# Attention and a gated feed-forward on one core: quadrants filled in the heads' order, the division of y and its parts spread over more steps, low halves summed at other steps

## The chip, the cores and the metric

The kernel runs on one core of a Trainium2 chip. A core has TensorE (PE in the profile), VectorE (DVE), ScalarE (ACT), GpSimd (POOL) and SyncE (SP), which issues DMAs. Every engine works through its own queue in order, and engines wait for each other on semaphores. The metric is the device time of one execution in microseconds (us), here the median of three runs.

## The reference

There are 4 batches of 1024 tokens with 256 channels, 16 heads of 16 channels, all in float32. The weights of attention are binarized: their signs times the mean of their absolute values per row.

```python
def _binlinear(x, W, b):
    Wb = _binarize(W)                    # mean(|W|) per row, times sign(W)
    return einsum('btc,oc->bto', x, Wb) + b
...
q, k, v = (split_heads(_binlinear(x, W, b)) for W, b in ((Wq, bq), (Wk, bk), (Wv, bv)))
att = softmax(einsum('bhtd,bhsd->bhts', q, k) * Dh ** -0.5)
y = einsum('bhts,bhsd->bhtd', att, v)    # heads joined to B, T, C
attention = _binlinear(y, Wp, bp)
...
h = silu(tlin(x, w1, s1)) * tlin(x, w2, s2)           # 256 -> 1024, ternary weights times a scale
h = gelu(tlin(h, h1, sh1))                            # 1024 -> 1024
h = gelu(tlin(h, h2, sh2))
ffn = tlin(h, w3, s3)                                 # 1024 -> 256
...
x = x + layernorm(attention(layernorm(x)))
x = x + layernorm(ffn(layernorm(x)))
```

## The kernel before

One program holds attention (`attention(True)`) and then the feed-forward part (`mlp`), which works in 8 blocks of 512 tokens and is not changed. A flag that `weight_jobs` computes tells whether the feed-forward weights have any low bits; for these inputs the short path runs.

**Blocks and steps.** A unit `u` is a batch and a group of four heads (16 units), a block is a unit and a half of its queries (512; 32 blocks, `blk`), and a block has 8 steps, one for each 128 keys. So there are 256 steps, `s`, and 10 steps ahead of them. In a step PE forms, for the four heads, the scores of the second pass (L664: three matmuls for each head, the third subtracts the row's maximum), the exponentials are taken by ACT (L674), and PE multiplies them by v (L690), in two groups of y matmuls. Beside this PE forms the scores of the first pass (L618, two matmuls per head), ten steps ahead, and DVE takes the maximum of each (L627). The four heads of a group stand in four quadrants of 32 partitions, so that their matmuls run side by side. A step is written as five slots. Head 0 and head 1 begin at slot 0, head 2 one slot later, head 3 three slots later (`BEGIN`). All scores go through seven PSUM banks (`through`), which `bank()` gives out by planned times.

**Jobs.** Everything else is a job that is put by hand at a place `(step, 0 or 1)`: 0 is issued after slot 2, 1 after the last slot. Jobs of one place are issued in the order in which they were placed. Those that matter here:

- `spread(u)` (L506), at step `16u - 16`: 24 DMAs on SP's queue bring q (high and low piece) and k of the next unit into the quadrants. They go quadrant by quadrant, in the order 2, 3, 0, 1. The unit's first pass begins six steps later. The spread of the first unit uses SP's and ACT's queues, before the steps begin.
- `fetch_y` (L705): ACT copies a block's y out of PSUM. `turn_y` (L710) transposes it on DVE, `divide` takes a reciprocal on DVE (L715) and multiplies on GpSimd (L716, into `yn`), `return_y` transposes back on DVE (L731) and issues four DMAs on SP into `yT`. They stand at steps 1 and 2 behind the block.
- `project_jobs(b, half)`: for each half batch, when its last heads are done. Two pieces (ACT takes the high part, L522, DVE the low part, L523), two projections (PE, L536; ACT's copy, L545; four GpSimd operations each, L550 and L551), four measured tiles (DVE, L162 and L163, the last with `rstd` on GpSimd, L151 and L153), and four finishing tiles (GpSimd, L565 and L568).
- `batch_jobs(b)`: measured tiles and norm tiles (GpSimd, L399) of the next batch, its transposes (L411, with L416 on ACT and L419 on DVE) and its values (L428, L434).
- `group_jobs(grp)`: the projections of q and k for two units (L469, L476), split into pieces by GpSimd (L482, L483).
- `combine` and `shift`: GpSimd arranges the maxima of a block (L636 to L638) for PE's transposes (L644).
- `weight_jobs`: 44 sums of low halves on GpSimd (`gather`, L817 and L818), each of a 128 x 512 piece of the feed-forward weights. For 28 of them SP loads the piece first, two ahead (L823): the load for the next but one waits until the piece has been read.

The places where these jobs come from:

```python
place((at - 6, 0), lambda u=u: spread(u))
...
at = (((b + 1) * NG - 1) * NQ + half + 1) * STEPS + (6, 10)[half]
...
at = (blk + 1) * STEPS + 1
...
while at % STEPS not in (3, 7) and job not in last_gathers:
```

Of the kernel before, what the change touches and what calls it, by code (L numbers as in the profile page):

```python
# [30 lines left out]
F32 = mybir.dt.float32  # L31
# [3 lines left out]
AF = mybir.ActivationFunctionType  # L35
ALU = mybir.AluOpType
# [10 lines left out]
def sandwich_kernel(  # L47
# [23 lines left out]
    nc = tc.nc  # L71
    B, T, C = x.shape
    F = w1T.shape[1]
    KC = C // P
    NF = F // P
    DH = C // HEADS
    NG = HEADS // 4
    NT = T // P
    NQ = T // 512
# [76 lines left out]
    def moments(n, tag):  # L156
        return scratch[-1].tile([P, n, 2], F32, tag=f"mvp{n}", name=f"mvp_{tag}")
# [73 lines left out]
    def attention(signs):  # L231


        with ExitStack() as actx:
# [11 lines left out]
            def bank():  # L246
                b = min(free_at, key=free_at.get)
                clock["PE"] = max(clock["PE"], free_at.pop(b))
                return b
# [105 lines left out]
            STEPS = NT  # L355
# [21 lines left out]
            def half_tile(name, dtype=F32):  # L377

                return a2.tile([P, NT // 2, C], dtype, tag="xn", name=name, bufs=3)
# [109 lines left out]
            def spread(u, queues=(nc.sync,)):  # L489

                grp, i = divmod(u, 2)
                q_of[u] = [
                    a2.tile([P, T], F32R, tag=f"qs{n}", name=f"qs{n}_{u}") for n in range(2)
                ]
                k_of[u] = a2.tile([P, T], F32R, tag="ks", name=f"ks_{u}")
                for g in (2, 3, 0, 1):
                    rows = slice(64 * i + 16 * g, 64 * i + 16 * g + 16)
                    for half in range(2):
                        to = slice(32 * g + 16 * half, 32 * g + 16 * half + 16)
                        for dst, src in (  # L500
                            (q_of[u][0], pieces_of[grp, True][0]),
                            (q_of[u][1], pieces_of[grp, True][1]),
                            (k_of[u], pieces_of[grp, False][half]),
                        ):
                            queue = queues[half % len(queues)]
                            queue.dma_start(dst[to, :].bitcast(F32), src[rows, :].bitcast(F32))  # L506
# [3 lines left out]
            def project_jobs(b, half):  # L510

                y_pieces, y_by = [], []

                def piece(k):

                    if k == 0:
                        y_pieces[:] = [half_tile(f"y{j}_{b}_{half}", F32R) for j in range(2)]
                    hi, lo = (
                        y.rearrange("p n c -> p (n c)")[:, bass.ts(k, 512)] for y in y_pieces
                    )  # L520
                    y, factor = yT_of[b, half][:, k, :], alpha_sb[:, 2, k : k + 1]
                    y_by.append(nc.scalar.activation(hi, y, AF.Copy, scale=factor).ins)  # L522
                    y_by.append(nc.vector.scalar_tensor_tensor(  # L523
                        lo, y, factor, hi.bitcast(F32), ALU.mult, ALU.subtract
                    ).ins)

                def project(m):
                    t = bank()
                    ys = [
                        y.rearrange("p n c -> p (n c)").rearrange("p (k t) -> p k t", k=KC)  # L530
                        for y in y_pieces
                    ] if signs else [yT_of[b, half]]
                    for i in range(2):
                        for k in range(KC):
                            for j, y in enumerate(ys):
                                put(t, nc.tensor.matmul(  # L536
                                    through[:, t, bass.ts(i, C)],
                                    y[:, k, bass.ts(2 * m + i, P)], w_in["p"][:, k, :],
                                    start=(k == 0 and j == 0),
                                    stop=(k == KC - 1 and j == PIECES - 1),  # L540
                                ), y_by)
                    if m == 0:
                        z_of[b, half] = half_tile(f"z_{b}_{half}")
                    z = z_of[b, half][:, 2 * m : 2 * m + 2, :]
                    got([t], "ACT", nc.scalar.copy(  # L545
                        z, through[:, t, :].rearrange("p (n c) -> p n c", n=2)
                    ))
                    for i in range(2):
                        if signs:
                            nc.gpsimd.tensor_mul(z[:, i, :], z[:, i, :], az_bc)  # L550
                        nc.gpsimd.tensor_add(z[:, i, :], z[:, i, :], bz_bc)  # L551

                def measure_tile(i):
                    if i == 0:
                        z_of["moments"] = moments(NT // 2, f"z{b}_{half}")
                    mv = z_of["moments"]
                    measure_one(mv, i, z_of[b, half][:, i, :], f"z{b}_{half}")
                    if i == NT // 2 - 1:
                        z_of["moments"] = mv, rstd(mv[:, :, 1], NT // 2, f"z{b}_{half}")

                def finish_tile(i):
                    z = z_of[b, half][:, i, :]
                    to = x_sb[:, b, half * NT // 2 + i, :]
                    mv, rs = z_of["moments"]
                    nc.gpsimd.tensor_scalar(  # L565
                        z, z, mv[:, i, 0:1], rs[:, i : i + 1], ALU.subtract, ALU.mult
                    )
                    nc.gpsimd.tensor_add(to, to, z)  # L568

                return [lambda k=k: piece(k) for k in range(KC) if signs], [  # L570
                    lambda m=m: project(m) for m in range(2)
                ], [
                    lambda i=i: measure_tile(i) for i in range(NT // 2)
                ], [lambda i=i: finish_tile(i) for i in range(NT // 2)]
# [160 lines left out]


            jobs = {}

            def place(at, job):
                jobs.setdefault(at, []).append(job)  # L740

            first = -STEPS - LEAD
            for b in range(1, B):
                norms, turns, values = batch_jobs(b)
                at = b * NG * NQ * STEPS + first
                for i, job in enumerate(norms):
                    place((at - 32 + i // 2, i % 2), job)
                for i, job in enumerate(turns):
                    place((at - 18 + i // 2, i % 2), job)

                for i, job in enumerate(values):
                    place((at - first - STEPS + 3 + 2 * i, 0), job)
            for u in range(1, B * NG):
                at = u * NQ * STEPS + first
# [3 lines left out]
                place((at - 6, 0), lambda u=u: spread(u))  # L758
            for b in range(B):
                for half in range(2 if b < B - 1 else 1):  # L760
                    at = (((b + 1) * NG - 1) * NQ + half + 1) * STEPS + (6, 10)[half]
                    pieces, projects, measures, finishes = project_jobs(b, half)
                    for i, job in enumerate(pieces):
                        place((at - 2, i), job)
                    for i, job in enumerate(projects):
                        place((at + i, 1), job)
                    for i, job in enumerate(measures):
                        place((at + 3 + i // 2, i % 2), job)
                    for i, job in enumerate(finishes):
                        place((at + 5 + i, 0), job)  # L770

            *tile_jobs, turn = middle_input()
            for n in range(8):
# [6 lines left out]
            for blk in range(BLOCKS):  # L780
                at = (blk + 1) * STEPS + 1
                hurry = blk == BLOCKS - 1
                for job, when in (
                    (turn_y, (at, 1)), (divide, (at + 1, 0)), (return_y, (at + 1, 1))
                ):
                    when = (total, 1) if hurry else when
                    place(when, lambda blk=blk, job=job: job(blk))
# [64 lines left out]
            loads, gathers, last_gathers = weight_jobs()  # L852
# [14 lines left out]
            at = 44  # L867
            for job in gathers + last_gathers:
                if job is last_gathers[0]:
                    at = max(at, free + 6)  # L870
                while at % STEPS not in (3, 7) and job not in last_gathers:
                    at += 1
                place((at, 1), job)
                at += 1
# [55 lines left out]
            for s in range(first, total + 1):  # L930
                steps = slots(s)
                for i, (some, parts) in enumerate(steps):
# [3 lines left out]
                    at = clock["PE"]  # L936
# [358 lines left out]
    with small_ones.Else():  # L1295
        attention(False)
        mlp("G", True, wp_all)
# [43 lines left out]
```

## Time and profile before

| | |
|---|---|
| median of three runs | 1618.42 us (1615.15 to 1619.83) |
| the profiled execution | 1616.46 us, its span 1614.6 us |
| mean granted TensorE clock | 0.982 |
| TensorE, VectorE, ScalarE, GpSimd busy | 95%, 67%, 51%, 26% |
| L627, maxima on VectorE | 1024 of 680 ns, 642.8 us |
| L674, exponentials on ScalarE | 1024 of 604 ns, 546.9 us |
| L710 and L731, transposes of y on VectorE | 32 of 704 and 32 of 702 ns |
| L716, the division on GpSimd | 32 of 619 ns |
| L817 and L818, a sum of low halves on GpSimd | 44 of 610 and 1281 ns |
| L506, DMAs of the spreads on SP's queue | 372, landing after 2.4 us (median) |

A line of a timeline gives the start and the length in us, the engine, the line of the kernel, the operation, what it writes and reads, how often in a row, and in brackets how long the engine stood idle before it and what ended that. A line of the list of waits gives who waited for whom, the total in us, how many times, and the longest. A line of a table of stretches gives the stretch, its length, the busy time of PE, PE's weight loads, DVE, ACT and POOL, the granted clock, the DMA share and GB/s.

### The profile page before, as it was taken

How to read it: one execution, taken by the hardware profiler on the slowest of the kernel's cores; microseconds unless marked ns; L12 is line 12 of the kernel's file. 1: busy time of each engine (PE TensorE's matmuls, PEld its weight loads, DVE VectorE, ACT ScalarE, POOL GpSimd, SP SyncE). 2: the span in 40 equal slices, each digit the busy share in tenths (PEclk: the TensorE clock that was granted, in tenths of full speed). 3: DMA queues.
4: the chain of work that ended last, by engine and by line, in shares of the span. 5: the costliest groups of instructions: out<-in, count | busy, mean ns of one | idle time of the engine just before them, and what ended most of it. 6: DMA issues, size and time to landing. Idle time of an engine off the chain costs nothing.

```text
span 1614.6 us, 31662 instructions
## 1 busy us (share of the span) xinstructions
PE 1533.2 (95%) x12964; PEld 982.4 (61%) x12964; DVE 1074.6 (67%) x1964; ACT 822.8 (51%) x1481; POOL 427.9 (26%) x574
## 2 busy tenths in 40 slices
PE   4599999998999999999989999999999999999997
PEld 3354444543445444444434468888888888888886
DVE  4588878888887888887879743644545454545443
ACT  2067677676777667776767771223232323232221
POOL 1011322565132555325631142120202020202011
PEclk9689999999999999999999999999999999999999
DMA  1502332212221232132123003000000000000000
GB/s 56 108 3 46 66 90 47 44 27 64 57 60 35 57 64 59 32 73 60 27 54 96 8 10 128 1 13 1 14 1 14 1 14 1 13 1 14 1 13 16
DMA packets 35707, 60.11 MB, mean 37 GB/s; under 512 B 10208, under 2 KB 21728, under 8 KB 35552
## 3 DMA queue, kind: packets, MB, share of 16 engines
q1 hardware_dynamic: 29568, 44.35, 12.9%
q0 software_dynamic: 3792, 11.54, 2.4%
q10 hardware_dynamic: 2192, 2.10, 0.6%
q8 instruction: 104, 1.70, 0.4%
q14 instruction: 51, 0.42, 0.1%
HBM read 24.40 MB, written 4.19 MB: 18 GB/s over the span
## 4 chain that ended last, share of the span: by engine, by line
PE 78%; DVE 8%; POOL 5%; ACT 4%; SPq 2%; issue 2%; DMA 1%; ACTq 0%; DVEq 0%
PE g L1075 29%; PE y L690 12%; PE through L664 11%; PE through L618 9%; PE p L1075 7%; DVE nm L627 5%; PE fzp L1189 4%; PE through L469 2%; ACT e L674 2%; SPq L506 2%; PE through L428 1%; PE through L644 1%; POOL z L565 1%; POOL xn L399 1%; PE through L536 1%
## 5 line engine op out<-in xcount | busy, mean ns | idle before, releaser
L627 DVE TENSOR_REDUCE nm<-through 128x1 f32<-128x512 f32 x1024 | 642.8, 680 | 127.9 <-PE through L618 66.7
L674 ACT ACTIVATE e<-through 128x512 f32<-128x512 f32 x1024 | 546.9, 604 | 182.9 <-PE through L664 168.2
L618 PE MATMUL through<-ks,qs 32*128 32x512 f32 x2048 | 467.3, 450 | 22.8 <-DMA ks<-h1b_sb 17.5
L664 PE MATMUL through<-qs,ks 32*128 32x512 f32 x2048 | 446.5, 439 | 21.7 <-DVE nm L627 16.2
L664 PE MATMUL through<-nmT,ones_r 32*128 32x512 f32 x1024 | 352.2, 454 | 0.4 <-ACT nmT L651 0.4
L690 PE MATMUL y<-e,v 128*32 128x256 f32 x4096 | 324.1, 394 | 0.0
L618 PEld LDWEIGHTS through<-ks,qs 32*128 32x128 f32 x2048 | 218.7, 187 | 127.8 <-issue 81.9
L664 PEld LDWEIGHTS through<-qs,ks 32*128 32x128 f32 x2048 | 206.2, 185 | 52.7 <-DVE nm L627 28.1
L1075 PE MATMUL g<-g,h_sb 128*128 128x512 f32 x1024 | 235.7, 390 | 0.0
L1075 PEld LDWEIGHTS g<-g,h_sb 128*128 128x128 f32 x1024 | 191.7, 188 | 39.5
L664 PEld LDWEIGHTS through<-nmT,ones_r 32*128 32x128 f32 x1024 | 139.6, 184 | 92.4 <-issue 89.5
L690 PEld LDWEIGHTS y<-e,v 128*32 128x32 f32 x4096 | 86.5, 108 | 171.1 <-issue 151.7
L1118 ACT ACTIVATE g2f<-g,sh_sb 128x512 f32<-128x512 f32 x64 | 44.2, 691 | 200.4 <-PE g L1075 173.0
L1118 ACT ACTIVATE g1f<-g,sh_sb 128x512 f32<-128x512 f32 x64 | 44.1, 691 | 170.1 <-PE g L1075 166.8
L151 POOL TENSOR_SCALAR ve_fz<-mvp_fz 128x4 f32<-128x4 f32 (+1 forms) x8 | 1.9, 233 | 470.7 <-DVE mvp_fz L163 470.7
L1075 PE MATMUL g<-h,h1a_sb 128*128 128x512 f32 x512 | 126.4, 389 | 0.0
L1075 PE MATMUL g<-h,h1b_sb 128*128 128x512 f32 x512 | 126.4, 389 | 0.0
L1045 DVE CAST g<-g2f 128x512 fp32r<-128x512 f32 x64 | 27.7, 433 | 142.0 <-ACT g2f L1118 142.0
L1075 PE MATMUL p<-xnT_sb,w_sb 128*128 128x512 f32 x512 | 118.0, 390 | 1.7 <-DVE hf L1151 1.7
L1075 PEld LDWEIGHTS p<-xnT_sb,w_sb 128*128 128x128 f32 x512 | 95.5, 188 | 22.0 <-DVE hf L1151 2.1
L1075 PEld LDWEIGHTS g<-h,h1b_sb 128*128 128x128 f32 x512 | 96.1, 188 | 20.0
L1075 PEld LDWEIGHTS g<-h,h1a_sb 128*128 128x128 f32 x512 | 96.1, 188 | 19.9
(173 smaller groups left out, 1486.5 us busy)
## 6 DMA issues: line engine op xcount, KB each, us to landing
qs<-h1b_sb SPq DMA_DIRECT2D x248, 64.0 KB, 2.4
ks<-h1b_sb SPq DMA_DIRECT2D x124, 64.0 KB, 2.4
wraw<-in_dram SPq DMA_DIRECT2D x28, 256.0 KB, 2.9
h_sb<-in_dram POOLq DMA_DIRECT2D x4, 1024.0 KB, 8.2
yT<-yt SPq DMA_DIRECT2D x112, 32.0 KB, 2.0
out_dram<-x_sb SPq DMA_DIRECT2D x7, 512.0 KB, 2.8
x_sb<-in_dram SPq DMA_DIRECT2D x3, 1024.0 KB, 5.6
w_sb<-in_dram POOLq DMA_DIRECT2D x3, 1024.0 KB, 7.7
```

The lines of the kernel that those rows point to most:

```text
L399: engine.tensor_scalar(xn_of[half][:, i, :], x_sb[:, b, half * NT // 2 + i, :], mv[:, i, 0:1], rs[:, i : i + 1], ALU.subtract, ALU.mult,)
L469: put(t, nc.tensor.matmul(through[:, t, :], w_in[tag][:, k, bass.ts(c, P)], xnT[i][:, k, bass.ts(j, 512)], start=(k == 0 and i == 0), stop ...
L506: queue.dma_start(dst[to, :].bitcast(F32), src[rows, :].bitcast(F32))
L618: put(t, nc.tensor.matmul(through[:, t, :], q_of[u][n][rows, bass.ts(qt, P)], k_of[u][rows, bass.ts(j, 512)], start=(n == 0), stop=(n == 1),))
L627: got([t], "DVE", nc.vector.tensor_reduce(nm_of[blk][:, n4, j, g : g + 1], through[:, t, :], AX.X, ALU.max, negate=True))
L664: t, nc.tensor.matmul(through[:, t, :], lhs, rhs, start=(n == 0), stop=(n == 2)),
L674: exps.append(got([t], "ACT", nc.scalar.activation(e_of[s, g], through[:, t, :], AF.Exp)))
L690: nc.tensor.matmul(y_of[blk][32 * g : 32 * g + 32, cols], v_sb[n // 2][:, n % 2, :, :].rearrange("p h d -> p (h d)")[:, bass.ds((4 * g4 + ...
L1045: nc.vector.tensor_copy(hi, full)
L1075: nc.tensor.matmul(out[c], wk, src[j][:, k, :], start=(k == 0 and i == 0 and j == 0), stop=(k == n_k - 1 and i == len(ws) - 1 and j == 1),)
L1118: nc.scalar.activation(g, ps, AF.Gelu, scale=scale[:, c : c + 1])
L1189: nc.tensor.matmul(out_ps[i][:, :C], g2[j][:, k, bass.ts(i, P)], wk, start=(k == 0 and n == 0 and j == 0), stop=(k == NF - 1 and n == len( ...
```

## The change

The spreads fill the quadrants in the order 0, 1, 2, 3. The high and the low piece of y become jobs of their own, half a step apart, and all jobs of a half batch stand one step later. `turn_y` stands half a step later, `divide` half a step, `return_y` a whole step. The sums of low halves go to steps 0, 4 and 7 of eight instead of 3 and 7, but to none of the steps that are marked as busy: those with norm tiles, with finishing tiles, and those that follow a projection. No operation is added or removed.

```diff
-                for g in (2, 3, 0, 1):
+                for g in range(4):
...
-                def piece(k):
-
-                    if k == 0:
+                def piece(k, low):
+
+                    if k == 0 and not low:
                         y_pieces[:] = [half_tile(f"y{j}_{b}_{half}", F32R) for j in range(2)]
...
-                    y_by.append(nc.scalar.activation(hi, y, AF.Copy, scale=factor).ins)
-                    y_by.append(nc.vector.scalar_tensor_tensor(
-                        lo, y, factor, hi.bitcast(F32), ALU.mult, ALU.subtract
-                    ).ins)
+                    if low:
+                        y_by.append(nc.vector.scalar_tensor_tensor(
+                            lo, y, factor, hi.bitcast(F32), ALU.mult, ALU.subtract
+                        ).ins)
+                    else:
+                        y_by.append(nc.scalar.activation(hi, y, AF.Copy, scale=factor).ins)
...
-                return [lambda k=k: piece(k) for k in range(KC) if signs], [
+                return [
+                    (k + low, lambda k=k, low=low: piece(k, low))
+                    for k in range(KC if signs else 0) for low in range(2)
+                ], [
...
+            busy = set()
...
                     place((at - 32 + i // 2, i % 2), job)
+                    if i >= NT // 2:
+                        busy.add(at - 32 + i // 2)
...
-                    at = (((b + 1) * NG - 1) * NQ + half + 1) * STEPS + (6, 10)[half]
+                    at = (((b + 1) * NG - 1) * NQ + half + 1) * STEPS + (7, 11)[half]
                     pieces, projects, measures, finishes = project_jobs(b, half)
-                    for i, job in enumerate(pieces):
-                        place((at - 2, i), job)
+                    for i, job in pieces:
+                        place((at - 2 + i // 2, i % 2), job)
                     for i, job in enumerate(projects):
                         place((at + i, 1), job)
+                        busy.add(at + i + 1)
...
                     for i, job in enumerate(finishes):
                         place((at + 5 + i, 0), job)
+                        busy.add(at + 5 + i)
...
-                    (turn_y, (at, 1)), (divide, (at + 1, 0)), (return_y, (at + 1, 1))
+                    (turn_y, (at + 1, 0)), (divide, (at + 1, 1)), (return_y, (at + 2, 1))
...
-                while at % STEPS not in (3, 7) and job not in last_gathers:
+                while (at % STEPS not in (0, 4, 7) or at in busy) and job not in last_gathers:
                     at += 1
```

## The prediction

> **What bounds the kernel.** I read the busy shares and the chain of waits on the page, then the timelines of TensorE (PE) and VectorE (DVE), then the list of waits.
>
> ```profile
> PE 1533.2 (95%) x12964; PEld 982.4 (61%) x12964; DVE 1074.6 (67%) x1964; ACT 822.8 (51%) x1481; POOL 427.9 (26%) x574
> ...
> PE 78%; DVE 8%; POOL 5%; ACT 4%; SPq 2%; issue 2%; DMA 1%; ACTq 0%; DVEq 0%
> ```
>
> The feed-forward part, from 956 us, keeps PE full and is not touched. Attention runs from about 55 to 956 us. Its unit is a step, which has two groups of y matmuls:
>
> ```profile
> 619.00 0.64 PE L690 MATMUL y<-e,v 128*32 128x256 f32 x8
> ...
> 621.70 0.64 PE L690 MATMUL y<-e,v 128*32 128x256 f32 x8
> ...
> 624.44 0.64 PE L690 MATMUL y<-e,v 128*32 128x256 f32 x8
> ```
>
> Between the last y groups of neighbouring steps lie 2.74 us: an undisturbed step, set by PE. I measured all 256 steps like this; every gain or loss below is a step's length less that of the same kind elsewhere. DVE is close behind:
>
> ```profile
> 621.80 2.48 DVE L627 TENSOR_REDUCE nm<-through 128x1 f32<-128x512 f32 x4 [0.42 <-PE through L618]
> 624.55 2.48 DVE L627 TENSOR_REDUCE nm<-through 128x1 f32<-128x512 f32 x4 [0.26 <-PE through L618]
> ```
>
> Four maxima take 2.48 us, so DVE has some 0.3 us free per step, just ahead of head 0's maximum. Work put there is cheap; work put behind head 1's maximum delays head 2's, whose PSUM bank PE needs back at once. So each block of eight steps has one of 3.26 us (the transpose of return_y, 0.70 us, after head 1's maximum: 0.52 lost), one of 3.34 (ACT's copy of y, L705, 0.61 us, delays the exponentials: 0.60) and one of 3.33 (the transposes of L644). The change can act on the first and on places where an engine waits:
>
> ```profile
> DVE y L523 <- ACT y L522: 14.2, 10, 7.3
> ...
> DVE yt L731 <- POOL yn L716: 13.3, 9, 3.0
> ```
>
> **Part 1: the division gets more steps.** Nothing is added; each block's turn_y, divide and return_y move by half a step, half a step and a whole one. The dearest place of before is this one, once in each of three batches:
>
> ```profile
> 806.25 1.22 POOL L565 TENSOR_SCALAR z<-z,mvp_z,rsp_z 128x256 f32<-128x256 f32 x1
> 807.56 0.73 POOL L568 TENSOR_TENSOR x_sb<-x_sb,z 128x256 f32<-128x256 f32 x1
> 808.28 1.21 POOL L565 TENSOR_SCALAR z<-z,mvp_z,rsp_z 128x256 f32<-128x256 f32 x1
> 809.58 0.72 POOL L568 TENSOR_TENSOR x_sb<-x_sb,z 128x256 f32<-128x256 f32 x1
> 810.26 0.62 POOL L716 TENSOR_TENSOR yn<-yt,r 128x256 f32<-128x256 f32 x1
> ...
> 810.91 0.71 DVE L731 STREAM_TRANSPOSE yt<-yn 128x512 f32<-128x512 f32 x1 [2.95 <-POOL yn L716]
> ...
> 812.25 0.79 PE L664 MATMUL through<-qs,ks 32*128 32x512 f32 x1 [3.11 <-DVE nm L627]
> ```
>
> GpSimd (POOL) works off four finishing tiles, 1.22 + 0.73 us each, ahead of the division; return_y's transpose blocks DVE, and the maxima behind it PE. The matmuls that follow last 0.79 us instead of 0.49. The three pairs of steps take 6.06 + 3.57, 6.74 + 2.99 and 8.11 + 3.81 us against 3.26 + 2.74: 3.6 + 3.7 + 5.9 = 13.3 lost. In the changed order the fourth tile stands behind the division. From the end of the step with the last measured tile POOL has 0.25 + 1.04 (rstd), at most one low-half sum of 0.61 + 1.28, three tiles of 1.95 and 0.62: 9.7 us, and return_y is issued four steps later, 2.74 + 3.34 + 2.74 + 2.74 = 11.6. The wait is gone: **-13.3** (from -6, if POOL is 2 us later than this, to -15).
>
> The clock over two such stretches:
>
> ```profile
> 361.00:373.00 12.00, 9.73 (x108) 3.87 (x100) 8.13 (x15) 5.48 (x11) 6.06 (x7) 0.86 0.66 146
> ...
> 806.00:820.00 14.00, 10.89 (x101) 4.23 (x102) 8.08 (x14) 5.30 (x10) 4.66 (x6) 0.76 0.73 150
> ```
>
> PE's gaps there are 2.27, 2.26 and 3.11 us, 7.6 together: what is lost beyond them is the granted clock (seventh number, 1.00 in undisturbed stretches). [...]
>
> Where eight measured tiles and POOL's norm tiles surround a division, L731 waits 1.28, 0.94 and 1.28 us (steps of 4.47, 4.12, 4.46 against 3.26): **-3.3**. POOL has one norm tile more ahead of the division (1.22), but return_y comes a step later (2.74).
>
> In plain blocks turn_y (0.70) now falls into DVE's free time, and the reciprocal (0.17 net) behind head 1's maximum; return_y costs the same 0.52 a step later. I take 0, bounds -0.2 to +0.8 per block (see the rivals). In four blocks return_y leaves the cover of a q/k projection (its PE time of 1.13 us, L469; the step there is 2.87, not 3.26): 4 x 0.4 = **+1.6** (0 to 2.1). In three it comes under the transposes of L411: **-1.0** (0 to -1.6). Its four DMAs (0.59 us each on SP's queue) pass no spread, only weight loads; their readers, the pieces, move one step too.
>
> **Part 2: pieces, projections, measured tiles.** The low piece no longer directly follows its high piece: the two waits of about 0.77 us per half go, but not DVE's 2 x 0.75 us. The steps are 3.92 against 2.74, and 4.50 against 3.84 with a projection, three of each. Two free times of 0.3 per half leave about 0.9 and, under a projection, 0.4: **-1.6** (0 to -5.5). The half-0 measured tiles, 2 x 0.6 us of DVE, leave the step in which a value matmul group (L428, 1.14 us of PE) covered them: 3 x 0.9 = **+2.7** (0 to 3.6).
>
> At the end of attention the last projection moves from step 255 to 256. There this is the chain:
>
> ```profile
> 945.19 0.73 POOL L550 TENSOR_TENSOR z<-z,az_bc 128x256 f32<-128x256 f32 x1 [13.62 <-ACT z L545]
> ...
> 951.21 0.62 POOL L716 TENSOR_TENSOR yn<-yt,r 128x256 f32<-128x256 f32 x1
> ...
> 955.91 2.34 PE L1075 MATMUL p<-xnT_sb,w_sb 128*128 128x512 f32 x9 [1.71 <-DVE hf L1151]
> ```
>
> Eight POOL operations, the last division, DVE's transpose and four measured tiles stand ahead of the first DVE work of the feed-forward part. All starts one step later, 1.97 to 2.13 us here, while PE's own work stays as long: the gap of 1.71 becomes 3.7. A gap over 2.27 brought the slow clock above (6.06 + 3.57 lost 3.63 with a gap of 2.27, so 1.4): **+3.4** (0 to 5).
>
> **Part 3: quadrants 0, 1, 2, 3.** Head 0 starts first, head 3 three fifths of a step later (1.6 us).
>
> ```profile
> 50.73 0.79 PE L618 MATMUL through<-ks,qs 32*128 32x512 f32 x1 [13.22 <-DMA ks<-h1b_sb]
> 54.83 2.37 PE L618 MATMUL through<-ks,qs 32*128 32x512 f32 x14 [3.31 <-DMA ks<-h1b_sb]
> ```
>
> Head 0 is served third and head 1 last. Turned round, three of the first step's maxima (0.6 us each) are done before the last landing: **-1.8** (0 to -2). Later PE waits for quadrant 1 in four steps, of 3.95, 3.38, 3.75 and 3.65 us against 2.74, by at most 1.2, less than head 3's 1.6: **-3.8** (-2 to -4). This also covers the three stretches that get shorter.
>
> **Part 4: low halves.** The same 44 sums (1.9 us each), at other steps, none ahead of a division. A weight load issued behind a spread waits for 24 issues of 0.59 us: 14.2 + 2.9 to landing = 17 us, and is read seven steps (19 us) later. I cost it at 0. If that cover fails POOL waits some us, and behind it L636, which is due six steps of eight in.
>
> **Sum.** -13.3 - 3.3 + 1.6 - 1.0 - 1.6 + 2.7 + 3.4 - 1.8 - 3.8 = -17.1 us. The profiled execution took 1616.46 (span 1614.6, 1.86 around it), the median of the runs is 1618.42, 1.96 more. I predict 1618.42 - 17.1 = **1601**.
>
> **Rivals.**
> (a) Turn_y loses its cover. Before, it ran in the 0.60 us that PE waits for ACT's copy anyway. If its 0.70 does not fit the 0.3 us free, every block pays 0.65 + 0.17 more: 31 x 0.8 = 25, so 1618.4 - 17.1 + 25 = **1626, slower**. For it: 0.70 > 0.3. Against: in that step PE is late, so DVE's queue is empty for longer. It decides from 17.1 / 31 = 0.55 us per block.
> (b) The division is still late: with the sum at the step before the finishing tiles, POOL's 1.9 us of margin is gone in two of three batches, and half of the 13.3 comes back: **1608**. For it: POOL waits for DVE's measured tile first. Against: the sum of rows above.
> (c) The quadrants' order does nothing, as all four must land anyway: 5.6 come back: **1607**. Against: PE started at 50.73 on one quadrant with another outstanding.
> (d) The losses stay hidden and the pieces cost nothing: -17.1 - 1.6 - 2.7 - 3.4 - 3.9 = -28.7: **1590**.
>
> **Chances.** Forecast 0.55, (a) 0.12, (b) 0.13, (c) 0.09, (d) 0.11. A difference under 0.3% (4.9 us) can't be told from none. Slower: two thirds of (a), 0.08; same: the rest of (a), and (b) with (c) or larger losses, 0.10; faster 0.82. The range, 1590 to 1614, reaches from (d) past (b) and (c) with a part of (a).
>
> **What will show it.** L731's wait for POOL falls from 13.3 to under 4 us; the clock is 1.00 in the three stretches; no L618 waits for a quadrant after 84 us; L523's wait falls below 10; PE's last gap before L1075 grows to about 3.7. I am wrong if the blocks' 3.26 and 3.34 steps add up to more than before, or a wait of L636 or L817 appears in PE's chain.

## The result

The changed kernel takes 1608.85 us, the median of five runs (1606.13 to 1610.78), against 1618.42 (1615.15 to 1623.09): a ratio of 0.9937, 95% interval 0.9914 to 0.9961. That is 9.6 us less. The prediction was 17.4 less, 1601, with a range of 1590 to 1614. The profiled execution of after took 1606.13 us, its span 1604.1, 10.5 less than before. In after, most lines of the attention steps stand 2 to 5 lower than before (L716 is L721, L731 is L736), those from the jobs of the weights on 10 lower (L862 is L872, L1075 is L1085).

First the busy times and the chain of waits on the page of after:

```profile
PE 1532.5 (96%) x12964; PEld 981.6 (61%) x12964; DVE 1076.4 (67%) x1964; ACT 821.7 (51%) x1481; POOL 429.4 (27%) x574
...
PE 82%; DVE 9%; ACT 4%; SPq 1%; issue 1%; POOL 1%; DMA 1%; ACTq 0%; DVEq 0%; POOLq 0%
```

The work is the same, instruction for instruction. POOL's share of the chain fell from 5% to 1%. The list of waits of after (who waited for whom, us in total, times, longest):

```profile
DVE yt L736 <- POOL yn L721: 11.5, 3, 6.0
PE through L623 <- DMA ks<-h1b_sb: 11.3, 3, 7.7
...
DVE y L523 <- ACT y L527: 9.3, 1, 9.3
```

DVE's wait for the division was 13.3 in nine; it is 11.5 in only three, so one long wait is new. The two others, 0.7 and 4.8, are at the end of attention, where they were 0.7 and 1.7. PE's waits for quadrants are now all at the start. The low piece waits only once, at the end.

**The stretch that was dearest.** POOL's timeline where a half batch's finishing tiles meet a division, third batch (before, this stood at 806 us):

```profile
785.14 1.23 POOL L567 TENSOR_SCALAR z<-z,mvp_z,rsp_z 128x256 f32<-128x256 f32 x1
...
788.03 1.22 POOL L567 TENSOR_SCALAR z<-z,mvp_z,rsp_z 128x256 f32<-128x256 f32 x1
789.33 0.74 POOL L570 TENSOR_TENSOR x_sb<-x_sb,z 128x256 f32<-128x256 f32 x1
790.05 1.22 POOL L567 TENSOR_SCALAR z<-z,mvp_z,rsp_z 128x256 f32<-128x256 f32 x1
791.36 0.73 POOL L570 TENSOR_TENSOR x_sb<-x_sb,z 128x256 f32<-128x256 f32 x1
792.57 0.62 POOL L721 TENSOR_TENSOR yn<-yt,r 128x256 f32<-128x256 f32 x1 [0.48 <-DVE r L720]
793.17 1.23 POOL L567 TENSOR_SCALAR z<-z,mvp_z,rsp_z 128x256 f32<-128x256 f32 x1
```

The division stands ahead of the fourth tile, as forecast, and POOL even stands idle for 0.48 us ahead of it, until the reciprocal comes. Its result is there at 793.19, and return_y's transpose starts at 795.0 without a wait. The effect on PE is seen from the first and the third of these stretches in the table of stretches (busy PE, weight loads, DVE, ACT, POOL, clock, DMA share, GB/s):

```profile
361.00:373.00 12.00, 11.96 (x144) 5.45 (x144) 11.45 (x24) 8.87 (x17) 3.39 (x7) 1.00 0.53 134
...
785.00:799.00 14.00, 13.71 (x172) 5.98 (x168) 13.14 (x23) 9.76 (x19) 9.25 (x11) 1.00 0.70 159
```

PE is busy for 11.96 of 12 us instead of 9.73, at a clock of 1.00 instead of 0.86.

**The new wait.** After, at 847 us, all engines but PE's matmuls:

```profile
846.10 0.59 SPq L506 DMA_DIRECT2D ks<-h1b_sb  x1
847.73 0.66 POOL L872 DMA_DIRECT2D h1b_sb<-in_dram  x1 [20.16 <-DMA qs<-h1b_sb]
848.42 0.63 POOL L721 TENSOR_TENSOR yn<-yt,r 128x256 f32<-128x256 f32 x1
...
849.09 0.71 DVE L736 STREAM_TRANSPOSE yt<-yn 128x512 f32<-128x512 f32 x1 [6.03 <-POOL yn L721]
```

L872 loads weights of the second feed-forward layer into `h1b_sb`, the buffer from which the last spread takes q and k. So it waits until that spread, 24 issues on SP's queue, has read its source. It is issued on POOL's queue, at place 0 of step 226, and the division of block 27 stands right behind it: POOL runs the two in that order (847.73 and 848.42 us), so a multiplication of 0.63 us waits for SP's DMAs, DVE's transpose 6.03 us for the multiplication, and the maxima behind that transpose, and PE, for DVE. Before, the division was issued at the same place but ahead of this load, which alone sat out the wait (8.51 us); nothing that PE needed then stood behind it:

```profile
861.05 0.62 POOL L716 TENSOR_TENSOR yn<-yt,r 128x256 f32<-128x256 f32 x1 [11.46 <-DVE r L715]
870.18 2.27 POOL L862 DMA_DIRECT2D h1b_sb<-in_dram  x4 [8.51 <-DMA ks<-h1b_sb]
```

The stretch of after in the table of stretches:

```profile
840.00:860.00 20.00, 13.85 (x152) 5.71 (x148) 11.43 (x21) 8.76 (x17) 3.47 (x8) 0.83 0.61 149
```

PE lacks 6.15 us of work, and then runs with a lower clock (0.83 over the stretch). Steps 227 and 228 take 11.15 + 2.98 us; before they took 2.74 + 2.75: 8.65 lost, more than the whole difference between forecast and result.

**Where the time went**, measured step by step as in the prediction (before to after, profiled executions, us):

| place | forecast | measured |
|---|---|---|
| three pairs with finishing tiles ahead of the division (steps 82-83, 146-147, 210-211) | -13.3 | -3.6, -3.7, -5.9 = -13.3 |
| norm tiles around a division (25-27, 89-91, 153-155) | -3.3 | -1.54, -1.52, -1.52 = -4.6 |
| plain blocks | 0 | 3.26 + 2.74 became 2.78 + 3.23: 0 |
| four blocks that leave a q/k projection (11, 43, 107, 171) | +1.6 | +0.53, +0.58, +0.61, +0.59 = +2.3 |
| three blocks under the transposes of L411 (34, 98, 162) | -1.0 | -0.48, -0.49, -0.48 = -1.45 |
| pieces and measured tiles, half 0 (59-67 and so on) and half 1 (71-79) | +1.1 | +2.7 and -0.9 = +1.8 |
| end of attention (253-254, and after the last y) | +3.4 | -1.07 + 5.12 = +4.0 |
| quadrants, later steps (37, 117, 133, 197) | -3.8 | -1.10, -0.64, -0.97, -0.91 = -3.6 |
| start, up to the first y | -1.8 | -2.8 |
| **load ahead of the division (227-228)** | none | **+8.65** |
| all other steps | none | -1.5 |

### The profile page after: what moved, and what is told of

Its sections match the earlier page's. It is cut to its first block, busy times and chain, and to the rows that moved or that the text cites. A ratio compares the mean times of both kernels' runs of the same rounds, so it can differ in the third digit from the quotient of the medians.

```text
span 1604.1 us, 31764 instructions
## 1 busy us (share of the span) xinstructions
PE 1532.5 (96%) x12964; PEld 981.6 (61%) x12964; DVE 1076.4 (67%) x1964; ACT 821.7 (51%) x1481; POOL 429.4 (27%) x574
## 4 chain that ended last, share of the span: by engine, by line
PE 82%; DVE 9%; ACT 4%; SPq 1%; issue 1%; POOL 1%; DMA 1%; ACTq 0%; DVEq 0%; POOLq 0%
PE g L1085 29%; PE y L695 14%; PE through L669 12%; PE through L623 9%; PE p L1085 7%; DVE nm L632 6%; PE fzp L1199 4%; PE through L469 2%; ACT e L679 2%; SPq L506 1%; PE through L428 1%; PE through L649 1%; PE through L538 1%; PE through L411 1%; DVE yt L736 1%
## 5 line engine op out<-in xcount | busy, mean ns | idle before, releaser
L669 PE MATMUL through<-qs,ks 32*128 32x512 f32 x2048 | 445.2, 436 | 17.4 <-DVE nm L632 8.3
L1085 PE MATMUL g<-g,h_sb 128*128 128x512 f32 x1024 | 235.7, 390 | 0.0
L1085 PEld LDWEIGHTS g<-g,h_sb 128*128 128x128 f32 x1024 | 191.7, 188 | 39.5
L1085 PE MATMUL g<-h,h1b_sb 128*128 128x512 f32 x512 | 126.4, 389 | 0.0
L1085 PE MATMUL g<-h,h1a_sb 128*128 128x512 f32 x512 | 126.4, 389 | 0.0
L1085 PE MATMUL p<-xnT_sb,w_sb 128*128 128x512 f32 x512 | 119.5, 394 | 3.7 <-DVE hf L1161 3.0
L1085 PEld LDWEIGHTS p<-xnT_sb,w_sb 128*128 128x128 f32 x512 | 96.6, 190 | 24.2 <-DVE hf L1161 3.4
L1085 PEld LDWEIGHTS g<-h,h1a_sb 128*128 128x128 f32 x512 | 96.1, 188 | 20.0
L1085 PEld LDWEIGHTS g<-h,h1b_sb 128*128 128x128 f32 x512 | 96.1, 188 | 19.9
```

Of the source, the lines that this page charges most:

```text
L669: t, nc.tensor.matmul(through[:, t, :], lhs, rhs, start=(n == 0), stop=(n == 2)),
L1085: nc.tensor.matmul(out[c], wk, src[j][:, k, :], start=(k == 0 and i == 0 and j == 0), stop=(k == n_k - 1 and i == len(ws) - 1 and j == 1),)
```

## The experiments

Every ratio is to the kernel before, run on the same chip beside it. Differences of steps and spans are those of one profiled execution each. In the expectations, e1 is the kernel with the load behind the division, e2 that one with the old end of attention besides, and e7 and e8 are the first two kernels of part 5.

**1. The load behind the division, and the old order at the end.** The first run is the changed kernel with the loads into `h1b_sb` one place later:

```diff
-                    (free + NQ * STEPS + 2 + i, 0), lambda to=to, i=i: nc.gpsimd.dma_start(
+                    (free + NQ * STEPS + 2 + i, 1), lambda to=to, i=i: nc.gpsimd.dma_start(
```

> The changed kernel with the four weight loads into h1b (L872) issued at the second place of their steps, behind the division instead of ahead of it. Theory: in the changed kernel the first of these loads waits on GpSimd's queue for the last spread to have read its source, and the division of that block stands behind it; step 227 then takes 11.15 us instead of 2.74. With the load behind the division step 227 should take about 3.2 us like its kind, and the span should fall by 8.4 to 8.7 us, to about 1595.5. Rival: the long step comes from the late quadrants of the last spread themselves, or from DVE's transposes in this block; then the span stays within 2 us of 1604.1.

1601.14 us, ratio 0.9894 (0.987 to 0.9917). POOL's timeline:

```profile
842.32 0.62 POOL L721 TENSOR_TENSOR yn<-yt,r 128x256 f32<-128x256 f32 x1 [13.01 <-DVE r L720]
850.36 2.26 POOL L872 DMA_DIRECT2D h1b_sb<-in_dram  x4 [7.42 <-DMA qs<-h1b_sb]
```

The load still waits, now behind the division, and nobody waits for it. Steps 227 and 228 take 3.22 + 2.74, 8.2 less than in after. The span (1597.6) is only 6.5 shorter, since this execution's first y came 1.0 later and its step 1 was 0.56 longer.

The mirror image takes the kernel before and puts only its first load half a step earlier, ahead of the division:

```diff
-                    (free + NQ * STEPS + 2 + i, 0), lambda to=to, i=i: nc.gpsimd.dma_start(
+                    (free + NQ * STEPS + 2 + i - (i == 0), int(i == 0)), lambda to=to, i=i: nc.gpsimd.dma_start(
```

> The kernel before with only the first weight load into h1b issued half a step earlier, so that it stands ahead of the division of its block on GpSimd's queue, as the change has made it. Theory: the division, DVE's transpose and PE wait for the landing of the last spread: 8 to 10 us longer, a span of about 1623 to 1625, all of it in the steps 226 to 228. Rival: GpSimd's wait is covered, as it was before, and the span stays within 2 us of 1614.6.

1626.8 us, ratio 1.0061 (1.0038 to 1.0084). POOL and DVE in the timeline:

```profile
867.12 0.66 POOL L862 DMA_DIRECT2D h1b_sb<-in_dram  x1 [19.55 <-DMA qs<-h1b_sb]
867.82 0.63 POOL L716 TENSOR_TENSOR yn<-yt,r 128x256 f32<-128x256 f32 x1
868.48 0.71 DVE L731 STREAM_TRANSPOSE yt<-yn 128x512 f32<-128x512 f32 x1 [8.13 <-POOL yn L716]
```

Steps 226 and 227 take 13.29 + 3.34 instead of 3.25 + 2.74, 10.6 more; the span rises by 8.6 only, since this execution's first y came 1.6 earlier. So the order of these two instructions costs 8 to 11 us of steps in either kernel, added or taken away, with everything else as it was. That is shown from both sides.

The next run is the first one with the end of attention at its old place:

```diff
-                    at = (((b + 1) * NG - 1) * NQ + half + 1) * STEPS + (7, 11)[half]
+                    at = (((b + 1) * NG - 1) * NQ + half + 1) * STEPS + ((7, 11)[half] if b < B - 1 else 6)
...
+                early = blk == BLOCKS - 2
                 for job, when in (
+                    (turn_y, (at, 1)), (divide, (at + 1, 0)), (return_y, (at + 1, 1))
+                ) if early else (
                     (turn_y, (at + 1, 0)), (divide, (at + 1, 1)), (return_y, (at + 2, 1))
```

> The kernel of e1, and the last half batch of attention (its pieces, projections, measured and finishing tiles, and the division of the block before the last) back at the places of before. Theory: the end of attention loses 4 us because GpSimd's eight operations on z start a step later and everything that the feed-forward part's first DVE work waits for stands behind them; PE's last gap before the feed-forward matmuls should fall from 2.95 to about 1.7 us, the matmuls behind it should run at full clock, and the span should be 3.5 to 4.5 us below e1. Rival: the gap is set by the table load and ACT's gates, which do not move; then the span stays within 1 us of e1.

1598.91 us, ratio 0.9879 (0.9857 to 0.9901); span 1594.5, 3.1 less than the first run's. PE at the end of attention, after and then this run:

```profile
934.76 5.68 PE L1085 MATMUL p<-xnT_sb,w_sb 128*128 128x512 f32 x24 [0.72 <-ACT z L547]
943.39 3.01 PE L1085 MATMUL p<-xnT_sb,w_sb 128*128 128x512 f32 x7 [2.95 <-DVE hf L1161]
```

```profile
928.18 5.73 PE L1088 MATMUL p<-xnT_sb,w_sb 128*128 128x512 f32 x24
935.65 6.65 PE L1088 MATMUL p<-xnT_sb,w_sb 128*128 128x512 f32 x28 [1.74 <-DVE hf L1164]
```

The gap of 2.95 is 1.74 again, and PE no longer waits 0.72 for ACT's copy of the projection moved behind the last step. After the gap of 2.95, seven matmuls take 3.01 us, 0.43 each; after 1.74 it is 6.65 for 28, 0.24 each: the slow clock (granted 0.50 from 943.9 to 947.2 us in after). The time after the last y falls by 4.8, steps 253 and 254 take 1.1 more: 3.7 net.

**2. The quadrants alone.** The kernel before with `range(4)` in place of `(2, 3, 0, 1)`:

> The kernel before with the quadrants' order 0, 1, 2, 3 alone. Theory: 2.8 us at the start, as three maxima of the first step are done before the last quadrant lands, and 3.6 us in the four steps that wait for a quadrant: the span falls by 6 to 7 us, to about 1608. Rival: all quadrants must land anyway and the steps gain nothing, or only the start does: 0 to 3 us.

1613.34 us over twelve runs, ratio 0.9972 (0.9957 to 0.9987): 4.5 less, with 2.4 either way. The span fell by 3.3. The four later steps give -0.69, -0.64, -1.02 and -0.46, together -2.8. The first y came 1.2 earlier, of which step 1 took 0.45 back. So the span's 3.3 lies between the theory and the rival: the steps did gain, the start hardly. Of the other steps three differ by more than 0.5, and they show the clock at work. The gap at step 26 is 1.28 us in this run and 1.27 in the kernel before, below, of the same cause (DVE waiting for the division):

```profile
171.00:178.00 7.00, 5.72 (x56) 2.20 (x53) 5.07 (x8) 3.21 (x6) 3.79 (x4) 0.76 0.09 21
583.00:592.00 9.00, 6.76 (x88) 2.75 (x81) 6.39 (x12) 4.73 (x9) 5.35 (x7) 1.00 0.59 102
```

```profile
171.00:178.00 7.00, 5.73 (x73) 2.53 (x72) 5.63 (x10) 3.95 (x9) 4.51 (x5) 1.00 0.09 21
```

The same PE time in 7 us holds 56 matmuls instead of 73, at a clock of 0.76 instead of 1.00; steps 26 and 27 take 1.5 longer. At step 146 it is the other way round: a gap of 2.24 us keeps its clock here (1.00 from 583 to 592 us), and one of 2.26 lost it before (0.83 from 586 to 596 us), 1.6 in this run's favour. In both places the gap is nearly the same with and without the edit and only the clock behind it differs, so this is put down to the executions and not to the edit.

**3. The division's own steps, without the rest.** The changed kernel with turn_y, divide and return_y where they were:

```diff
-                    (turn_y, (at + 1, 0)), (divide, (at + 1, 1)), (return_y, (at + 2, 1))
+                    (turn_y, (at, 1)), (divide, (at + 1, 0)), (return_y, (at + 1, 1))
```

> The changed kernel with turn_y, divide and return_y back at the places of before; everything else as changed. Theory: most of the 13.3 us at steps 82, 146 and 210 come from the finishing tiles' later place, which puts the fourth of them behind the division, so they do not come back: from the last measured tile GpSimd has 0.25 + 1.04, a sum of 1.89 in two of three batches, three tiles of 1.95 and 0.62, together 9.7 us, and return_y would come after 8.8: waits of about 1 us in steps 82 and 146 and none in 210. Steps 226 to 228 lose their 8.2 us (the weight load is behind the division again), steps 25 to 27 of the norm tiles lose 1.5 each, the four blocks with q/k projections win 0.5 each: a span of about 1599. Rival: the later division alone frees those steps; then 82, 146 and 210 are again 3 us and more too long and the span is 1606 or more.

1610.82 us, ratio 0.9969 (0.9951 to 0.9986); span 1609.1, 5.0 more than after's. Half of this theory fell, and its rival holds in part. The load costs nothing here, 8.65 less. But the three pairs of steps take 8.89, 7.40 and 6.45 us instead of 6.0 each: 4.7 come back. POOL at the first of them, and DVE:

```profile
357.17 0.61 POOL L827 CAST half<-h1a_sb 128x512 f32<-128x512 uint16 x1
357.86 1.29 POOL L828 TENSOR_TENSOR bits<-bits,half 128x512 f32<-128x512 f32 x1
359.13 1.24 POOL L567 TENSOR_SCALAR z<-z,mvp_z,rsp_z 128x256 f32<-128x256 f32 x1
...
365.18 0.62 POOL L721 TENSOR_TENSOR yn<-yt,r 128x256 f32<-128x256 f32 x1
```

```profile
365.83 0.71 DVE L736 STREAM_TRANSPOSE yt<-yn 128x512 f32<-128x512 f32 x1 [1.32 <-POOL yn L721]
```

A sum of low halves of 1.9 us stands ahead of the tiles in the first two batches, and there L736 waits 1.32 and 1.30; in the third, where none does, 0.35. The first pair lost 1.5 more than the second with the same wait; that this was the clock is an estimate, from the 1.5 us that steps 26 and 27 lost with it in experiment 2. So of the 13.3, 4.7 hang on the division's later place, and some 8.5 come without it. The 8.5 are put down to the finishing tiles' step later (three of them instead of four stand ahead of the division); no run moved those alone. Besides, the norm tiles' 4.6 return, and plain blocks are as long as with the late division, 3.26 + 2.74 against 2.78 + 3.23. The rest is not the edit's: the first y came 1.25 later and step 1 was 1.0 longer, and steps 26 and 72-73 lost 3 us, put down to the clock by the same estimate; after has a clock of 1.00 there (168 to 176 and 324 to 334 us).

**4. The old steps for the sums.** The changed kernel with `while at % STEPS not in (3, 7) and job not in last_gathers`:

> The changed kernel with the sums of low halves at steps 3 and 7 of eight, as before, also in the busy steps. Theory: the division now has room on GpSimd's queue with or without them, so the span stays within 3 us of 1604.1, and what is lost, if anything, is at steps 77 to 80, where a sum delays the last projection's z and with it the block's maxima. Rival: keeping the sums out of the busy steps is what freed the division; then GpSimd's division holds DVE up again at steps 82, 146 and 210 and the span rises by 6 us or more.

1608.44 us, ratio 0.9953 (0.9937 to 0.9968), against 0.9937 (0.9914 to 0.9961) for after. Its steps are those of after, except for step 1 (1.2 longer, at the start) and step 227 (0.6 shorter); L736 waits at none of the three places. With the division late, a sum ahead of the tiles is covered, here also in the third batch (787.58 us): the new rule for the sums is worth nothing that these runs can tell.

**5. Taking the good parts.** The next kernel keeps the load behind the division, moves half 0's jobs back one step, and gives the old places to the end of attention and to the blocks whose return_y had lost the cover of a projection or of value matmuls:

```diff
+                    at = (((b + 1) * NG - 1) * NQ + half + 1) * STEPS + ((6, 11)[half] if b < B - 1 else 6)
...
+                early = blk in (0, 4, 12, 20) or blk % 8 in (6, 7)
```

> The kernel of e1 with the places of before where the changed kernel lost cover: the half-0 jobs, the division in their two blocks, in the four blocks with q/k projections, and at the end. Theory: beside the end (4 us, as in e2) 2.7 us at steps 59 to 67 and 2.2 us at steps 11, 43, 107 and 171 come back: 4 to 5 us below e2's span of 1594.5, about 1590. Rival: these differences are not costs of the new places but follow PE's clock or the banks; then the span stays within 2 us of e2's.

1587.62 us, ratio 0.9826 (0.9802 to 0.985); span 1587.6, 6.9 less than the run with the old end. The four blocks give -0.53, -0.60, -0.61 and -0.60, 2.3 together, and half 0 gives 1.8 in each of three batches, 5.4: more than the 2.7 that moving it had cost: with its old place and the pieces parted it is 0.9 a half faster than before.

DVE in a plain block of this kernel, and below of the next, which puts return_y half a step later still, ahead of head 0's maximum, in 14 blocks (`(at + 3, 0)` for `(at + 2, 1)`, not in the early blocks and not in 3, 8, 11, 16, 19 and 24):

```profile
465.47 0.70 DVE L736 STREAM_TRANSPOSE yt<-yn 128x512 f32<-128x512 f32 x1
466.10 3.75 DVE L632 TENSOR_REDUCE nm<-through 128x1 f32<-128x512 f32 x6
```

```profile
464.79 0.70 DVE L736 STREAM_TRANSPOSE yt<-yn 128x512 f32<-128x512 f32 x1
465.41 2.44 DVE L632 TENSOR_REDUCE nm<-through 128x1 f32<-128x512 f32 x4
468.11 2.48 DVE L632 TENSOR_REDUCE nm<-through 128x1 f32<-128x512 f32 x4 [0.25 <-PE through L623]
```

> The kernel of e7 with return_y in 14 blocks at the first place of the step after, that is, ahead of head 0's maximum instead of behind head 1's. Theory: DVE has 0.3 us free there, so of the transpose's 0.63 us only about half reaches PE: the steps of 3.23 us become 2.9 or less, 14 x 0.35 = 5 us in all. Rival: the transpose costs the same 0.5 us wherever it stands, and the span stays within 1.5 us of e7's.

1585.28 us, ratio 0.9807 (0.9783 to 0.9831), the lowest median of all and 31 us less than before on the same chip. From the kernel ahead of it (0.9826) the times alone can't tell it; the steps can. In the first of the two views six maxima follow the transpose without a pause, DVE being behind; in the second it has caught up after four. Thirteen of the 14 steps are shorter by 0.27 to 0.38 us, 3.9 together, where 5 were expected. But the span fell only by 1.2, chiefly because two stretches lost the clock, 1.5 us each; this is the first of them:

```profile
536.00:546.00 10.00, 9.14 (x85) 3.82 (x81) 7.67 (x13) 6.88 (x14) 4.65 (x5) 0.83 0.11 29
```

```profile
541.00:551.00 10.00, 9.15 (x97) 4.76 (x101) 8.78 (x16) 7.14 (x14) 5.20 (x6) 1.00 0.09 29
```

The second line is the same stretch in after. PE has the same gap of 0.85 us in both (high and low piece and a projection in one step, 136), and the same busy time, but 85 matmuls instead of 97: 1.5 us, at a clock of 0.83. The last run spreads the four pieces of each half over more places, so that these gaps go:

> The kernel of e8 with the low pieces of y (L523) ahead of head 0's maximum too, each in a step of its own, and those of the second half two steps earlier. Theory: in the changed kernel the first low piece of the second half stands behind head 1's maximum and PE stands idle for 0.85 us in each of steps 72, 136 and 200; this idle time goes, and with it the 1.5 us that the slower clock behind it cost in two of the three in e8, and the low pieces of the first half cost about 0.3 us less: 2 to 6 us in all, a span of 1580 to 1584. Rival: the low piece's 0.75 us is too long for DVE's 0.3 us of free time and the loss only moves to the steps before: within 1.5 us of e8's 1586.4.

1587.19 us, ratio 0.9811 (0.9784 to 0.9839): no gain. The gaps of 0.85 are gone, the longest left is 0.59, but steps 61, 70, 71 and 72 of the first batch are 0.16, 0.34, 0.14 and 0.13 longer, and the clock dropped all the same, once, at step 200. So the rival holds: the loss moved to the steps before. PE at step 200:

```profile
752.84 0.50 PE L669 MATMUL through<-qs,ks 32*128 32x512 f32 x1 [0.24 <-ACT e L679]
753.59 0.74 PE L623 MATMUL through<-ks,qs 32*128 32x512 f32 x1 [0.26 <-DVE nm L632]
```

Behind two gaps of 0.24 and 0.26 the matmuls' length goes from 0.50 to 0.74.

## Why the prediction was right and where it was wrong

**Direction, range and mechanism held; the size was 1.8 times too large, by one missing term.** The step that failed is the queue check in Part 1. The prediction followed return_y's DMAs past the weight loads on SP's queue and asked only of the sums whether they come ahead of a division. It did not ask it of the loads that POOL issues, though the division moves on POOL's queue. One of those stood at the place the division was moved past, with a wait of 8.51 us in the trace of before that cost nothing there. Without it, the kernel takes 0.9894 of the time before (0.987 to 0.9917): 17.2 less, where 17.1 was the sum. That they agree so closely is luck: the interval is 13 to 21 us, and in the table the other places add up to -19.2, with misses both ways.

Of the signs named in advance, the clock of 1.00 in the three stretches, the end of the later waits for quadrants and L523's wait (9.3) came true. The wait of the transposes for POOL did not fall below 4 us: it is 11.5, of which 6.0 are the new wait. The last gap of PE grew to 2.95 and not to 3.7.

**Part 1, the large terms.** The 13.3 came back whole, at a clock of 1.00. The margin of 1.9 us that was worked out (9.7 against 11.6) was 1.36 in the first two batches, where a sum stands ahead of the tiles; in the third, shown above, it was 1.8, but with no sum: there the issue of another load (0.84 us, at 787.13) and the wait for the reciprocal filled the time. Of the 13.3, 4.7 hang on the division's move, as experiment 3 showed; the prediction gave it to the order of the tiles and the extra step without parting them. The norm tiles gave 4.6, not 3.3: the steps with the wait gave 3.0, and the step before them, where turn_y stood among the measured tiles, another 1.6 that was not counted (3.51, 3.85 and 3.50 became 3.08). The projection's cover cost 2.3, not 1.6, and the transposes gave 1.45, not 1.0; both times the whole of the 0.5 to 0.6 that return_y costs was lost or hidden, not the 0.4 and 0.33 taken.

**Rival (a), turn_y without cover,** is refuted: the step with turn_y and the reciprocal takes 2.78 us, 0.04 over an undisturbed one, in all plain blocks. So 0.70 + 0.17 us of DVE's work cost next to nothing there, though DVE's free time is only 0.3; what covers the rest was not parted.

**Part 2** was off by little: +1.8 for +1.1. The sign of each item held (half 0 loses, half 1 gains). But the cover of the value matmuls was lost by return_y too: step 59 fell from 3.92 only to 3.26, and with the division at its old place (experiment 3) it is 2.74. Steps 60 to 67 together became 1.55 longer; which of their jobs has what share was not parted. Experiment 5 shows that half 0 is better off with its old step and the pieces parted.

**The end** cost 4.0, for 3.4. The gap grew to 2.95, not 3.7, since part of the delay shows up as the 0.72 that PE waits for ACT's copy.

**Part 3.** The later steps gave 3.6 of 3.8 in this pair, 2.8 in the kernel with the quadrants alone. PE's start in after:

```profile
44.43 0.76 PE L623 MATMUL through<-ks,qs 32*128 32x512 f32 x1 [7.66 <-DMA ks<-h1b_sb]
...
53.56 2.07 PE L623 MATMUL through<-ks,qs 32*128 32x512 f32 x10 [2.33 <-DMA ks<-h1b_sb]
```

The 2.8 up to the first y agrees with the 1.8 by luck. Two runs with one and the same order, the old one, had their last quadrant 1.6 us apart (54.79 and 53.19). Counted from that landing, the ninth maximum begins after 7.90 us in all runs with the new order and after 9.27 in both with the old: 1.37 gained. That is the three maxima of 0.6, less the 0.4 by which DVE's first maximum behind the landing comes later. By the end of step 1, however, the old order needs 39.2 and the new one 38.6 in the mean (37.15 to 39.08): with PE's low clock there (over 76 to 94 us 0.62 in before, 0.72 in after, 0.56, 0.62 and 0.55 with the old end of attention, in the mirror image and with the old steps for the sums), most of it is gone again.

**Part 4** cost 0, as taken; no wait of the sums entered PE's chain, and PE's one wait for `combine`, 2.0 us at the start, is as long as before. But "none ahead of a division" does not hold: in the first two batches a sum still runs ahead of the tiles and the division (351.40 us in the first). Rival (b), the division late behind a sum, did not occur in after, and experiments 3 and 4 show when it would: with the division at its old place. Rival (c) holds for the start at most. Of (d) nothing was seen.

## What to carry to other kernels

When a job moves in an engine's queue, list every instruction of that queue which it passes, DMA issues first, and ask for each what it waits for: a wait that costs nothing in one profile, because nothing stands behind it, is a trap at the next place. Look for such waits in the list even where they are off the chain, as this one of 8.51 us was. Work parted into pieces should go where the engine in question has caught up; a move that is good for most blocks can be undone for those few that lose another cover by it.

## What the hardware showed beyond that

PE's granted clock fell after short gaps, and not always. A gap of 0.85 us in one step left the clock at 1.00 in after and was followed by 0.83 over 10 us in another kernel, 1.5 us lost; one of 1.28 was followed by 0.76 over 7 us with the quadrants alone, one of 1.27 by 1.00 in the kernel before; one of 2.24 left it at 1.00 over 9 us (quadrants alone), with one of 2.26 it was 0.83 over 10 us (before). With gaps of 2.95 us (0.50 from 943.8 to 947.2 us in after), 3.11 (0.76 from 806 to 820 us in before) and 6.15 (0.83 from 840 to 860 us in after) it fell too.

Narrower stretches of before and after show the pattern of these falls. The low clock is 0.50, for 3.4 us or for a multiple of that. In before it is 0.50 from 368.37 to 371.78 us, with 1.00 on both sides, from 590.23 to 593.65 and, for 6.83 us, from 812.10 to 818.93; in after for 10.24 us from 76.84 to 87.08, for 6.83 from 848.25 to 855.08, and for 3.41 from 943.82 to 947.23. The falls begin on a grid: in before at 78.24, 368.37, 590.23 and 812.10 us, 290.13, 221.86 and 221.87 apart, which are 85, 65 and 65 times 3.413 us (221.86 / 65); in after at 76.84, 848.25 and 943.82, 226 and 28 times 3.413 us apart. Which gap brings a fall is not told by that, since gaps of 0.85 and of 1.27 to 1.28 us went both ways. What decides it was not tried.

For a kernel this close to PE's limit (PE is busy for 96% of the span in after) it means that a single profile carries 1.5 us of luck for each such gap, and that sums of step lengths have to be read with the clock beside them.
